# A four-layer graph network on one core: how the Mamba scan gets its B and C rows and its carried state

## The chip, the cores and the metric

The kernel runs on one core of a Trainium2 chip. The metric is the time of one launch in device microseconds; the time before is 3810.78 us, the median of 3 runs (3806.26 to 3815.26). The core's engines run side by side, each through its own queue of instructions in order: TensorE (PE, with its weight loads shown as PEld), VectorE (DVE), ScalarE (ACT), GpSimd (POOL) and SyncE (SP), whose queue issues the DMAs. Semaphores tie the queues together: an instruction waits at the head of its queue until what it needs is there, and all behind it waits with it.

## The reference, cut to what matters

`x` is 3327 x 256, `adj` a sparse 3327 x 3327 matrix of weights. Four layers follow one another, the first three each as `x = layernorm(x + layer(x, adj))`. Layer 0 averages over neighbours and multiplies by W; layer 2 is graph attention; layer 3 makes two passes of diffusion and of attention cut to the top 90%. The change lies in layer 1 and at the seam to layer 2:

```python
h = relu(adj @ x @ gcn_w + gcn_b);  h = layernorm(h) * ln_g + ln_b
xz = h @ w_in;  xc, z = xz[:, :512], xz[:, 512:]
u = silu(causal_conv4(xc) + conv_b)
dbc = u @ w_xp                                   # 16 + 16 + 16 columns
dt = softplus(dbc[:, :16] @ w_dt + b_dt);  B = dbc[:, 16:32];  C = dbc[:, 32:]
dA = exp(dt[:, :, None] * -exp(A_log));  dBu = dt[:, :, None] * B[:, None, :] * u[:, :, None]
# along the 3327 rows:  hst = dA[t] * hst + dBu[t];  ys[t] = hst @ C[t]
y = (ys + u * D_skip) * silu(z);  return y @ w_out
```

The state has 512 channels times 16 states. For each state separately the recurrence is a linear scan along the rows, and `ys` is the sum over the 16 states of `h * C`.

## The kernel before, in words

The 3327 rows are padded to 26 row tiles of 128. Layer 1 has two streams that one program order weaves together.

**The convolution stream** (`convolve`, L254) makes `h` for one row tile after another: 26 matmuls of a 128x128 piece of the transposed adjacency (`at`, loaded nine pieces at a time through two buffers, L263) against all of x, then gcn_w, relu, and three small closures: `measure` (statistics on DVE, then power and nb on POOL, L249, L250, L292), `norm` (ACT, L295) and `turn` (PE transposes, ACT into `hT`, L306). It is a generator. Each `pump` runs one step of it, about nine matmuls, and a step also pops one waiting closure of the tile before.

**The scan** works on channels in the partitions and rows along the free axis, in eight chunks of 128, 256, 384 and five times 512 columns. `head(c)` (L359) makes u, the three-part copy of B and C, dt and du = dt * u for a chunk; it is a generator too and is drawn from during states 3 to 14 of the chunk before. Then, for each of 16 states:

- `decay` (L453): four ACT exponentials (L460) write dA for the four groups of 128 channels, in two buffers; POOL copies the carried state into column 0 of `db` (L458).
- `feed` (L463): one DVE multiplication db = du * B, 128x2048.
- `scan` (L468): one DVE scan over the four groups at once, each led by a column with dA = 0 and db = the carried state, so that it restarts there; POOL copies the last columns to `carry` (L476).
- the multiplication h * C on DVE (L549), with C in PSUM, and four PE matmuls by the identity (L557) that add the product to `ys` in PSUM.

The order on DVE is scan(s), feed(s+1), multiply(s). B and C lie in `dbc` with the state in the partition, while DVE needs them copied to all 128 partitions. The kernel does this on PE: B and C are split into three bf16 parts whose sum is the fp32 value (`parts`, L389, L393, L398, L407), and a matmul with a 0/1 selector `three` (L445 for B, two states ahead; L484 for C) adds the parts and spreads them. B goes by ACT from PSUM to SBUF (`row`, L448); C is read in PSUM. The row matmul, the projections (L355), the dt matmuls (L402), the transposes and the residual all share one PSUM pool of two buffers, `ps`.

After a chunk, `gate` (L491) multiplies `ys` by silu(z), and `back` (L493) multiplies by w_out, adds the residual X0 (L504) and normalizes the chunk's row tiles (POOL L249, L250, L509, L510; ACT L514). `values` (L335) then makes, per row tile, what layer 2 needs: the projection and `F`, the attention columns `col` (L347). For the last chunk all of `back` runs, then the remaining `values`.

Layer 2 (L675 to L757) takes `col`, makes exponentials (`q`, `eps`, `r`), and for each row tile loads two halves of `at` (L724), makes weights on DVE (L726, L729) and multiplies on PE (L732). A runtime branch stands ahead of it. Layer 3 follows; its pass 1 takes diffusion matmuls with `at` (L811, L813) and scores from q and k (L797).

Instructions are put into the engines' queues by a scheduler in program order with readiness, except where `keep_in_program_order` or `high_priority` stands; it also moves loads ahead where their buffers are free.

Of the kernel before, what the change touches and what calls it, by code (L numbers as in the profile page):

```python
# [18 lines left out]
P = 128  # L19
# [24 lines left out]
def gnn_kernel(ctx: ExitStack, tc: tile.TileContext, n: int, a: dict, out: bass.AP):  # L44
# [109 lines left out]
    with tc.tile_pool(name="l1b", bufs=1) as wpool, tc.tile_pool(name="l1at", bufs=2) as l1at:  # L154
# [33 lines left out]
        with tc.tile_pool(name="l1aw", bufs=1) as cwork, tc.tile_pool(name="l1c", bufs=2) as ch, \  # L188
                tc.tile_pool(name="l1t", bufs=3) as tmp, tc.tile_pool(name="l1s", bufs=2) as work, \
                tc.tile_pool(name="l1y", bufs=1, space=PSUM) as ypsum, \  # L190
                tc.tile_pool(name="l1p", bufs=2, space=PSUM) as psum, \
# [5 lines left out]
            w_dt = wpool.tile([6 * DS + DTR, DI], F32, name="w_dt")  # L197
            gb, one = w_dt[0:1, :D], w_dt[0:1, D:D + P]
# [19 lines left out]
            BC = 2 * DS  # L218
            w_sp = wpool.tile([P, NG, 3 * BC + DTR], F32, name="w_sp")
            nc.sync.dma_start(w_dt[3 * BC:, :], a["w_dt"])  # L220
            three = wpool.tile([3 * BC, BC], BF16, name="three")
            for k in range(3):
                nc.sync.dma_start(w_sp[:, :, k * BC:(k + 1) * BC], a["w_xp"][:, :, DTR:])
                nc.vector.tensor_copy(three[k * BC:(k + 1) * BC, :], ident[k * BC:(k + 1) * BC, k * BC:(k + 1) * BC])
            nc.sync.dma_start(w_sp[:, :, 3 * BC:], a["w_xp"][:, :, :DTR])

# [18 lines left out]
            hTs, us, szs, splits = {}, {}, {}, {}  # L245
# [6 lines left out]
            def convolve():  # L252
# [3 lines left out]
                for it in range(nt):  # L256
# [14 lines left out]
                    if rest:  # L271
                        rest.pop(0)()
                        full += 1
                    yield full
# [33 lines left out]
                    rest = [measure, norm, turn]  # L308
# [50 lines left out]
            def head(c):  # L359
# [3 lines left out]


# [20 lines left out]
                for g in range(NG):  # L385
                    nc.tensor.matmul(ps[:3 * BC + DTR, :w], w_sp[:, g, :], u[:, g, :],
                                     start=(g == 0), stop=(g == NG - 1))
                parts = splits[c] = ch.tile([3 * BC, WC], BF16, name="parts")[:, :w]
                nc.scalar.copy(parts, ps[:3 * BC, :w])  # L389
                left = scratch()[:3 * BC + DTR, 0, :w]  # L390
                nc.scalar.copy(left, ps[:3 * BC + DTR, :w])
                yield None
                nc.vector.tensor_sub(left[:3 * BC], left[:3 * BC], parts)  # L393
# [3 lines left out]
                for k in (1, 2):  # L397
                    nc.scalar.copy(parts[k * BC:(k + 1) * BC], left[k * BC:(k + 1) * BC])  # L398
                v, e = (scratch()[:, :, :w] for _ in range(2))
                for g in range(NG):  # L400
                    ps = psum.tile([P, WC], F32, name="ps")
# [174 lines left out]
            for _ in back(nch - 1):  # L576
                pass
# [785 lines left out]
```

## Time and profile before

| what | us |
|---|---|
| median of 3 runs | 3810.78 |
| profiled execution | 3813.28 |
| its span | 3811.5 |
| layer 1's scan: first scan starts | 406.5 |
| scans of chunks 1 to 7 start | 489.6, 603.0, 753.1, 934.5, 1116.5, 1298.7, 1473.1 |
| last multiplication by C ends | 1616.4 |
| first matmul of layer 2 | 1657.4 |
| first matmul of layer 3, pass 1 | 1994.5 |
| pass 2 | 2835.7 to the end |

The profile's lines of the timeline give start, duration, engine, source line, operation, output and inputs with their shapes, and in brackets how long the engine stood idle before and what released it. The table of stages gives the busy time of each engine in a stretch of the span, then the granted clock of TensorE, the busy share of the DMA engines and GB/s. The list of waits gives, for an engine and a line, who released it, total us, times and the longest one.

### The profile page before, as it was taken

Reading aid. Unit: us, or ns where it says so; the run is one execution under the profiler, and the core shown is the slowest. Engines: PE = TensorE matmul, PEld = TensorE weight load, DVE = VectorE, ACT = ScalarE, POOL = GpSimd, SP = SyncE. Lnnn points to the kernel's source line nnn. Section 1 sums busy time; section 2 is a strip of 40 time slices with the busy share of each in tenths; the row PEclk is TensorE's granted clock in tenths of the full one; section 3 lists DMA queues with packets and bytes.
Section 4 is the critical chain, followed back from the end, with each engine's and each line's share of the span. In section 5 each row is a group of like instructions: output and inputs, shape, how many; then the busy total and the mean of one; then the engine's idle time right before and its main releaser. Section 6 shows DMA issues by size and latency. Waiting matters only on the chain. (4 is left out here: it accounts for less than half of the span.)

```text
span 3811.5 us, 42006 instructions
## 1 busy us (share of the span) xinstructions
PE 3482.6 (91%) x15079; PEld 2570.3 (67%) x15079; DVE 2626.2 (69%) x5640; ACT 1739.7 (46%) x2612; POOL 497.9 (13%) x760
## 2 busy tenths in 40 slices
PE   8999999888989778689999999999999899999995
PEld 7888876554545334368877777777777676666764
DVE  1111588898989899957755444444442999999996
ACT  0000655554545465311113333333335878877773
POOL 0000122222212222111110000000000111111111
PEclk9999999998989888889999999999999999999997
DMA  7442221110111000034422221122112222222210
GB/s 230 144 136 96 78 64 50 43 42 31 42 36 43 12 0 0 0 133 141 149 90 74 63 60 52 55 63 60 53 55 61 64 65 61 63 63 61 63 51 7
DMA packets 115508, 252.99 MB, mean 66 GB/s; under 512 B 16450, under 2 KB 57410, under 8 KB 115154
## 3 DMA queue, kind: packets, MB, share of 16 engines
q1 hardware_dynamic: 115282, 250.14, 21.5%
q8 instruction: 122, 2.00, 0.2%
q14 instruction: 104, 0.85, 0.1%
HBM read 239.86 MB, written 10.22 MB: 66 GB/s over the span
## 5 line engine op out<-in xcount | busy, mean ns | idle before, releaser
L473 DVE TENSOR_TENSOR_SCAN h<-dA,db 128x2052 f32<-128x2052 f32 (+3 forms) x128 | 463.8, 3624 | 6.0 <-PE y L557 3.5
L460 ACT ACTIVATE dA<-dt,A_log 128x512 f32<-128x512 f32 (+3 forms) x512 | 296.3, 635 | 331.6 <-DVE h L473 277.8
L557 PE MATMUL y<-h,ident 128*128 128x512 f32 (+3 forms) x1024 | 436.9, 564 | 3.2 <-DVE h L549 3.2
L557 PEld LDWEIGHTS y<-h,ident 128*128 128x128 f32 x1024 | 200.7, 208 | 251.3 <-issue 225.6
L846 PE MATMUL acc<-G,wt 128*128 128x256 f32 x1352 | 345.7, 397 | 11.7 <-ACT wt L782 11.2
L846 PE MATMUL acc<-X,wt 128*128 128x256 f32 x1352 | 343.6, 391 | 8.3 <-ACT wt L844 8.0
L813 PE MATMUL acc<-F,at 128*128 128x256 f32 x1352 | 339.3, 380 | 1.7 <-ACT q L604 0.6
L846 PEld LDWEIGHTS acc<-G,wt 128*128 128x128 f32 x1352 | 247.2, 193 | 112.3 <-ACT wt L782 46.2
L116 PE MATMUL acc<-xa,at 128*128 128x257 f32 x1352 | 309.9, 383 | 5.8 <-DMA at<-in_adjT 5.7
L813 PE MATMUL acc<-X,at 128*128 128x256 f32 x1352 | 309.5, 382 | 3.0 <-issue 2.8
L846 PEld LDWEIGHTS acc<-X,wt 128*128 128x128 f32 x1352 | 242.5, 189 | 103.2 <-issue 41.3
L732 PE MATMUL acc<-F,at 128*128 128x257 f32 x1352 | 307.3, 384 | 4.9 <-DVE at L729 4.9
L264 PE MATMUL cb<-F,at 128*128 128x256 f32 x1352 | 309.6, 381 | 1.6 <-ACT hn L283 1.6
L466 DVE TENSOR_TENSOR db<-du,row 128x2048 f32<-128x2048 f32 (+3 forms) x128 | 240.0, 1878 | 84.3 <-ACT row L448 84.1
L858 DVE MAX8 cand<-e 128x8 f32<-128x128 f32 x676 | 142.1, 278 | 226.2 <-ACT e L799 214.6
L264 PEld LDWEIGHTS cb<-F,at 128*128 128x128 f32 x1352 | 256.5, 191 | 58.6 <-issue 17.6
L116 PEld LDWEIGHTS acc<-xa,at 128*128 128x128 f32 x1352 | 256.5, 191 | 43.3 <-issue 6.2
L732 PEld LDWEIGHTS acc<-F,at 128*128 128x128 f32 x1352 | 255.9, 192 | 41.6 <-issue 5.2
L813 PEld LDWEIGHTS acc<-X,at 128*128 128x128 f32 x1352 | 253.7, 191 | 43.2 <-issue 10.2
L813 PEld LDWEIGHTS acc<-F,at 128*128 128x128 f32 x1352 | 243.2, 190 | 39.2 <-issue 7.8
L549 DVE TENSOR_TENSOR h<-h,C 128x2048 f32<-128x2048 f32 (+3 forms) x128 | 240.8, 1881 | 38.2 <-PE C L484 25.2
L797 PE MATMUL sc<-kT,q 64*128 64x416 f32 x832 | 201.5, 561 | 37.7 <-ACT e L782 34.3
(308 smaller groups left out, 5320.0 us busy)
## 6 DMA issues: line engine op xcount, KB each, us to landing
at<-in_adjT SPq DMA_DIRECT2D x102, 832.0 KB, 4.5
at<-in_adjT SPq DMA_DIRECT2D x260, 320.0 KB, 3.0
at<-in_adjT SPq DMA_DIRECT2D x52, 576.0 KB, 3.7
at<-in_adjT SPq DMA_DIRECT2D x26, 512.0 KB, 3.6
xt<-in_xT SPq DMA_DIRECT2D x26, 128.0 KB, 4.1
qd<-q SPq DMA_DIRECT2D x104, 32.0 KB, 1.9
q<-qd SPq DMA_DIRECT2D x52, 64.0 KB, 1.9
at<-in_adjT SPq DMA_DIRECT2D x52, 64.0 KB, 1.8
```

The costliest lines, as they stand in the source:

```text
L116: nc.tensor.matmul(acc, at[:, j, :], rhs[:, j0 + j, :], start=(j0 + j == 0), stop=(j0 + j == nt - 1))
L264: nc.tensor.matmul(acc, at[:, j % JC, :], X0[:, j, :], start=(j == 0), stop=(j == nt - 1))
L460: nc.scalar.activation(dA[:, g, 1:], dt[:, g, :], AF.Exp, scale=A[:, g, s:s + 1])
L466: nc.vector.tensor_mul(by_group(dbs[s % 2], w)[:, :, 1:], du, B.to_broadcast([P, NG, w]))
L473: nc.vector.tensor_tensor_scan(h[:, :m], dAs[s % 2][:, :m], dbs[s % 2][:, :m], initial=0.0, op0=ALU.mult, op1=ALU.add)
L549: nc.vector.tensor_mul(h, h, C.to_broadcast([P, NG, w]))
L557: nc.tensor.matmul(ys[g][:, :w], ident, h[:, g, :], start=False, stop=(s == DS - 1))
L732: nc.tensor.matmul(acc, at[:, j, :], F[:, j0 + j, :], start=(j0 + j == 0), stop=(j0 + j == nt - 1))
L797: nc.tensor.matmul(pl[:, h, :w], q[k, :], kT[p][k, c0:c0 + w], start=True, stop=True)
L813: nc.tensor.matmul(acc, at[:, j, :], rhs[:, j0 + j, :], start=(j0 + j == 0), stop=(j0 + j == nt - 1))
L846: nc.tensor.matmul(acc, wt[:, j, :], rhs[:, j0 + j, :], start=(j0 + j == 0), stop=(j0 + j == nt - 1))
L858: nc.vector.max(cand[:, s * 8:(s + 1) * 8], z[:, s * SEG:(s + 1) * SEG])
```

## The change

1. **Rows.** `dbc` is copied once from PSUM to SBUF (`left`), and B and C are written to a DRAM tile. For each state one DMA fetches the state's B row and C row to all partitions, into one of three buffers (`lines`), issued two states ahead. The three-part split, the selector matmuls, the copy by ACT and the PSUM bank of C go; the shared PSUM pool has three buffers.
2. **Carried state.** `du` has one more column in front of each group, into which ACT copies the carried state; column 0 of the B row is 1, so that the feed writes it to `db`. ACT copies the last columns out. The scan works in place in `db`, which has three buffers.
3. **Weights of dt** stand four times at partitions 0, 32, 64, 96, and the dt matmuls go in pairs with high priority.
4. **Convolved tiles.** An empty closure is put in ahead of `norm`, and a fourth closure is popped per tile, behind the yield that follows the copy of `acc` (L270); norm comes one step later than before, and turn too.
5. **Last chunk.** Residual, statistics, power and normalization go by row tile, and `values` of the tiles before stand between.
6. **Layer 2.** The `at` pieces of row tile 0 have tiles of their own and are loaded ahead of the preparation; the pool has four buffers in place of five.

Cut to its core:

```diff
                 tc.tile_pool(name="l1y", bufs=1, space=PSUM) as ypsum, \
-                tc.tile_pool(name="l1p", bufs=2, space=PSUM) as psum, \
+                tc.tile_pool(name="l1p", bufs=3, space=PSUM) as psum, \
+                tc.tile_pool(name="l1d", bufs=1, space=DRAM) as l1d, \
                 tc.tile_pool(name="l1q", bufs=1, space=PSUM) as cpsum:
...
             nc.vector.memset(last, 0.0)
-            BC = 2 * DS
-            w_sp = wpool.tile([P, NG, 3 * BC + DTR], F32, name="w_sp")
-            nc.sync.dma_start(w_dt[3 * BC:, :], a["w_dt"])
-            three = wpool.tile([3 * BC, BC], BF16, name="three")
-            for k in range(3):
-                nc.sync.dma_start(w_sp[:, :, k * BC:(k + 1) * BC], a["w_xp"][:, :, DTR:])
-                nc.vector.tensor_copy(three[k * BC:(k + 1) * BC, :], ident[k * BC:(k + 1) * BC, k * BC:(k + 1) * BC])
-            nc.sync.dma_start(w_sp[:, :, 3 * BC:], a["w_xp"][:, :, :DTR])
+            w_sp = wpool.tile([P, NG, 32 * (NG - 1) + DTR], F32, name="w_sp")
+            nc.vector.memset(w_sp, 0.0)
+            for g in range(NG):
+                nc.sync.dma_start(w_dt[32 * g:32 * g + DTR, :P], a["w_dt"][:, g * P:(g + 1) * P])
+                nc.sync.dma_start(w_sp[:, :, 32 * g:32 * g + DTR], a["w_xp"][:, :, :DTR])
+            for k in range(2):
+                nc.sync.dma_start(w_sp[:, :, 32 * k + DTR:32 * k + DTR + DS],
+                                  a["w_xp"][:, :, DTR + k * DS:DTR + (k + 1) * DS])
...
                         rest.pop(0)()
+                    yield full
+                    if rest:
+                        rest.pop(0)()
                         full += 1
-                    yield full
                     for k in range(2):
...
                                                  scale=g1[:, k:k + 1], bias=b1[:, k:k + 1])
-                    rest = [measure, norm, turn]
+                    rest = [measure, lambda: None, norm, turn]
                     while it == 0 and rest:
...
                 for g in range(NG):
-                    nc.tensor.matmul(ps[:3 * BC + DTR, :w], w_sp[:, g, :], u[:, g, :],
+                    nc.tensor.matmul(ps[:w_sp.shape[2], :w], w_sp[:, g, :], u[:, g, :],
                                      start=(g == 0), stop=(g == NG - 1))
-                parts = splits[c] = ch.tile([3 * BC, WC], BF16, name="parts")[:, :w]
-                nc.scalar.copy(parts, ps[:3 * BC, :w])
-                left = scratch()[:3 * BC + DTR, 0, :w]
-                nc.scalar.copy(left, ps[:3 * BC + DTR, :w])
+                left = scratch()[:w_sp.shape[2], 0, :w]
+                nc.scalar.copy(left, ps[:w_sp.shape[2], :w])
+                bc = rows_of[c] = l1d.tile([2, DS, w], F32, name=f"bc{c}")
+                for k in range(2):
+                    nc.sync.dma_start(bc[k], left[32 * k + DTR:32 * k + DTR + DS])
                 yield None
-                nc.vector.tensor_sub(left[:3 * BC], left[:3 * BC], parts)
-                yield None
-                for k in (1, 2):
-                    nc.scalar.copy(parts[k * BC:(k + 1) * BC], left[k * BC:(k + 1) * BC])
                 v, e = (scratch()[:, :, :w] for _ in range(2))
-                for g in range(NG):
-                    ps = psum.tile([P, WC], F32, name="ps")
-                    nc.tensor.matmul(ps[:, :w], w_dt[3 * BC:, g * P:(g + 1) * P], left[3 * BC:],
-                                     start=True, stop=True)
-                    nc.scalar.activation(v[:, g, :], ps[:, :w], AF.Identity, bias=b_dt[:, g:g + 1])
-                    nc.scalar.activation(e[:, g, :], ps[:, :w], AF.Abs, bias=b_dt[:, g:g + 1])
-                yield None
-                nc.vector.tensor_sub(parts[2 * BC:], left[2 * BC:3 * BC], parts[2 * BC:])
+                for g0 in range(0, NG, 2):
+                    pair = [psum.tile([P, WC], F32, name="ps") for _ in range(2)]
+                    with tc.high_priority():
+                        for g, ps in enumerate(pair, g0):
+                            k = slice(32 * g, 32 * g + DTR)
+                            nc.tensor.matmul(ps[:, :w], w_dt[k, :P], left[k], start=True, stop=True)
+                    for g, ps in enumerate(pair, g0):
+                        nc.scalar.activation(v[:, g, :], ps[:, :w], AF.Identity, bias=b_dt[:, g:g + 1])
+                        nc.scalar.activation(e[:, g, :], ps[:, :w], AF.Abs, bias=b_dt[:, g:g + 1])
+                    yield None
                 nc.scalar.activation(e, e, AF.Exp, scale=-1.0)
...
                 nc.vector.scalar_tensor_tensor(dt, v, 0.0, e1, op0=ALU.max, op1=ALU.add)
-                du = ch.tile([P, NG, WC], F32, name="du", bufs=1)[:, :, :w]
-                nc.vector.tensor_mul(du, dt, u)
+                du = by_group(ch.tile([P, NG * (1 + WC)], F32, name="du", bufs=1), w)
+                nc.vector.tensor_mul(du[:, :, 1:], dt, u)
                 for g in range(NG):
...
                 nc.scalar.copy(szs[c][:, g, :], project(c, NG + g, w))
-            dAs, dbs = ([cwork.tile([P, NG * (1 + WC)], F32, name=f"{x}{i}") for i in range(2)] for x in ("dA", "db"))
+            dAs, dbs = ([cwork.tile([P, NG * (1 + WC)], F32, name=f"{x}{i}") for i in range(m)]
+                        for x, m in (("dA", 2), ("db", 3)))
             def by_group(t, w):
                 return t[:, :NG * (1 + w)].rearrange("p (g w) -> p g w", g=NG)
+            lines = [cwork.tile([P, 2, 1 + WC], F32, name=f"row{i}") for i in range(3)]
+            for r in lines:
+                nc.vector.memset(r[:, 0, 0:1], 1.0)
             def row(c, s):
-                parts = splits[c]
-                w = parts.shape[1]
-                pb = psum.tile([P, WC], F32, name="ps")[:, :w]
-                with tc.high_priority():
-                    nc.tensor.matmul(pb, three[:, s:s + 1].to_broadcast([3 * BC, P]), parts, start=True, stop=True)
-                B = work.tile([P, 1, WC], F32, name="row", bufs=2)[:, :, :w]
-                with tc.high_priority():
-                    nc.scalar.copy(B[:, 0, :], pb)
-                return B
+                w = us[c].shape[2]
+                r = lines[(c * DS + s) % 3][:, :, :1 + w]
+                nc.sync.dma_start(r[:, :, 1:], rows_of[c][None, :, s, :].to_broadcast([P, 2, w]))
+                return r
             def decay(x, s):
...
                 w = dt.shape[2]
-                dA, db = (by_group(x[s % 2], w) for x in (dAs, dbs))
+                dA = by_group(dAs[s % 2], w)
                 if s < 2 and (c == 0 or w != ends[c - 1] - starts[c - 1]):
                     nc.gpsimd.memset(dA[:, :, 0:1], 0.0)
-                nc.gpsimd.tensor_copy(db[:, :, 0], carry[:, s, :])
                 for g in range(NG):
                     nc.scalar.activation(dA[:, g, 1:], dt[:, g, :], AF.Exp, scale=A[:, g, s:s + 1])
+                nc.scalar.copy(du[:, :, 0], carry[:, s, :])
             def feed(x, s, B):
                 du = x[2]
-                w = du.shape[2]
-                nc.vector.tensor_mul(by_group(dbs[s % 2], w)[:, :, 1:], du, B.to_broadcast([P, NG, w]))
+                w = du.shape[2] - 1
+                tc.keep_in_program_order(nc.vector.tensor_mul(
+                    by_group(dbs[(x[0] * DS + s) % 3], w), du, B[:, 0:1, :].to_broadcast([P, NG, 1 + w])))
             def scan(x, s):
-                w = x[2].shape[2]
-                h = work.tile([P, NG * (1 + WC)], F32, name="h")
+                w = x[1].shape[2]
+                h = dbs[(x[0] * DS + s) % 3]
                 m = NG * (1 + w)
-                nc.vector.tensor_tensor_scan(h[:, :m], dAs[s % 2][:, :m], dbs[s % 2][:, :m],
+                nc.vector.tensor_tensor_scan(h[:, :m], dAs[s % 2][:, :m], h[:, :m],
                                              initial=0.0, op0=ALU.mult, op1=ALU.add)
                 h = by_group(h, w)
-                nc.gpsimd.tensor_copy(carry[:, s, :], h[:, :, w])
+                nc.scalar.copy(carry[:, s, :], h[:, :, w])
                 return h[:, :, 1:]
-            def reader(x, s):
-                parts = splits[x[0]]
-                w = parts.shape[1]
-                C = cpsum.tile([P, 1, WC], F32, name="C")[:, :, :w]
-                nc.tensor.matmul(C[:, 0, :], three[:, DS + s:DS + s + 1].to_broadcast([3 * BC, P]), parts,
-                                 start=True, stop=True)
-                return C
             def gate(c, ys):
...
                     nc.vector.tensor_mul(sz[:, g, :], ys[g][:, :sz.shape[2]], sz[:, g, :])
+            def residual(c, i):
+                it = starts[c] // P + i
+                po = psum.tile([P, WC], F32, name="ps")[:, :D]
+                for g in range(NG):
+                    nc.tensor.matmul(po, szs[c][:, g, i * P:(i + 1) * P], w_out[:, g, :],
+                                     start=(g == 0), stop=(g == NG - 1))
+                nc.vector.tensor_add(X[:, it, :], X0[:, it, :], po)
             def back(c):
-                sz = szs[c]
-                m = sz.shape[2] // P
+                m = szs[c].shape[2] // P
                 mv = small.tile([P, WC // P, 2], F32, name="mvc")
                 for i in range(m):
...
+                    residual(c, i)
+                    stats(mv[:, i, :], X[:, starts[c] // P + i, :])
                 rs = small.tile([P, WC // P], F32, name="rsc")
...
             decay(x, 0)
-            feed(x, 0, rows.pop(0))
-            C = reader(x, 0)
+            feed(x, 0, rows[0])
             ys = ahead = None
...
                     if nxt:
-                        feed(*nxt, rows.pop(0))
-                    nc.vector.tensor_mul(h, h, C.to_broadcast([P, NG, w]))
-                    if nxt:
-                        C = reader(*nxt)
+                        feed(*nxt, rows[1])
+                    nc.vector.tensor_mul(h, h, rows.pop(0)[:, 1:2, 1:].to_broadcast([P, NG, w]))
                     if s == 0:
...
             gate(nch - 1, ys)
-            for _ in back(nch - 1):
-                pass
+            for i in range(us[nch - 1].shape[2] // P):
+                it = starts[nch - 1] // P + i
+                residual(nch - 1, i)
+                mv = small.tile([P, 2], F32, name="mv")
+                stats(mv, X[:, it, :])
+                rs, nb = (small.tile([P, 1], F32, name=x) for x in ("rs", "nb"))
+                power(rs, mv[:, 1:2])
+                nc.gpsimd.tensor_scalar(nb, mv[:, 0:1], rs, -1.0, op0=ALU.mult, op1=ALU.mult)
+                nc.scalar.activation(X[:, it, :], X[:, it, :], AF.Identity, scale=rs, bias=nb)
+                while valued < ready:
+                    values()
+                ready = it + 1
             while valued < nt:
...
             fit = cpool.tile([1, 1], I32, name="fit")
+            ats = [cpool.tile([P, min(JH, nt - j0), P], F32, name=f"at{j0}") for j0 in range(0, nt, JH)]
+            for k, at in enumerate(ats):
+                nc.sync.dma_start(at, a["adjT"][0][:, k * JH:k * JH + at.shape[1], :])
             with tc.tile_pool(name="l2a", bufs=1) as wpool, \
...
                 with tc.tile_pool(name="l2", bufs=1) as pool, tc.tile_pool(name="l2w", bufs=2) as work, \
-                        tc.tile_pool(name="l2at", bufs=5) as atp, \
+                        tc.tile_pool(name="l2at", bufs=4) as atp, \
                         tc.tile_pool(name="l2p", bufs=3, space=PSUM) as psum:
...
                             m = min(JH, nt - j0)
-                            at = atp.tile([P, JH, P], F32, name="at")
-                            nc.sync.dma_start(at[:, :m, :], a["adjT"][it][:, j0:j0 + m, :])
+                            if it:
+                                at = atp.tile([P, JH, P], F32, name="at")
+                                nc.sync.dma_start(at[:, :m, :], a["adjT"][it][:, j0:j0 + m, :])
+                            else:
+                                at = ats[j0 // JH]
                             w = work.tile([P, JH, P], F32, name="w", bufs=1)
```

## The prediction, made before the changed kernel was run

> **What bounds the kernel now.** I read the table of stages first (busy time of each engine between the scan starts of the eight chunks), because the diff touches layer 1's scan and the two seams behind it. The whole span is no guide: PE is busy for 91% of it, but not here. Chunk 4 and the last chunk:
>
> ```profile
> 934.50:1116.50 182.00, 159.56 (x494) 90.49 (x494) 165.86 (x92) 92.94 (x148) 43.35 (x50) 0.93 0.13 38
> ...
> 1473.10:1616.40 143.30, 106.94 (x261) 51.19 (x259) 141.25 (x63) 60.57 (x118) 29.84 (x34) 0.88 0.00 0
> ```
>
> The columns are length, then PE, weight load, DVE, ACT, POOL. In chunk 4 DVE has the most work (165.86 of 182.00) and stands idle for 16.1 us; in the last chunk it is idle for 2. Over all eight (406.5 to 1616.4) the idle times are 29.8, 24.1, 18.9, 16.3, 16.1, 16.3, 10.4 and 2.1: 134 us. What ends them is in DVE's waits over that stretch:
>
> ```profile
> DVE db L466 <- ACT row L448: 84.1, 22, 12.9
> DVE h L549 <- PE C L484: 25.2, 10, 6.9
> DVE h L549 <- POOL carry L476: 9.2, 21, 1.6
> DVE h L473 <- PE y L557: 3.5, 4, 2.4
> ```
>
> The numbers are total us, times, longest. The first three, 118.5 us, wait for just what the change replaces. DVE's timeline shows the longest one, in chunk 4:
>
> ```profile
> 1062.05 2.29 DVE L549 TENSOR_TENSOR h<-h,C 128x2048 f32<-128x2048 f32 x1 [0.35 <-POOL carry L476]
> 1077.25 4.58 DVE L466 TENSOR_TENSOR db<-du,row 128x2048 f32<-128x2048 f32 x2 [12.92 <-ACT row L448]
> 1081.75 4.43 DVE L473 TENSOR_TENSOR_SCAN h<-dA,db 128x2052 f32<-128x2052 f32 x1
> ```
>
> The feed stood for 12.92 us. PE had only two shared PSUM buffers: ACT was at L404/L405 and waited for the dt matmuls L402, and the row's matmul got its buffer at 1075.96. Such a stall comes once per 512-column chunk with a head behind it. Undisturbed, the loop is DVE's alone, as in the last chunk:
>
> ```profile
> 1576.02 4.43 DVE L473 TENSOR_TENSOR_SCAN h<-dA,db 128x2052 f32<-128x2052 f32 x1
> 1580.36 2.27 DVE L466 TENSOR_TENSOR db<-du,row 128x2048 f32<-128x2048 f32 x1
> 1582.71 2.29 DVE L549 TENSOR_TENSOR h<-h,C 128x2048 f32<-128x2048 f32 x1
> 1584.91 4.43 DVE L473 TENSOR_TENSOR_SCAN h<-dA,db 128x2052 f32<-128x2052 f32 x1
> ```
>
> 8.90 us from scan to scan, and the change keeps those three instructions.
>
> **Rows by DMA.** Removed from PE: 16 row and 16 C matmuls per chunk, 437 + 411 ns at 512 columns (13.6 us; 11.4, 9.7 and 7.2 in chunks 2, 1, 0). From ACT: 16 row copies of 0.58 and three casts (.564 + 2 x .615), 11.1 us. From DVE: two subtractions, 1.36. Put in: per chunk two small writes to DRAM, and per state one broadcast read of 2 rows to 128 partitions, 512 KB in packets of 2 KB. No row of before shows this transfer. From below: 256 packets on 16 engines at the 88 ns that 2 KB packets took are 1.4 us; from above, the loads of 512 KB landed after 3.6 us, 832 KB after 4.5, a broadcast of 128 KB after 4.4 to 5.1. I take 4. It is issued two states ahead, when mult(s-1) frees its buffer: up to feed(s+2) there lie scan, feed, mult, scan, 4.35 + 2.34 + 2.20 + 4.35 = 13.2 us (a quarter of it at 128 columns, by the sizes, where PE is the bound). So it hides, with 9 us over. DMA engines were .10 to .13 busy here; 54.5 MB are added. On SP's queue the rows stand among convolve's `at` loads; By SP's waits it stood there 439 us for a free buffer, 32.6 at the longest, and a row issued behind such a wait is late. That stays as a range end.
>
> By this the 84.1 and the 25.2 us go. What is late next is ACT.
>
> **Carry on ACT.** Removed: POOL's copies. Added to ACT: two copies 128x4 per state; nearest row is ACT's copy 128x2, 161 ns, so 0.16 to 0.2, 6.4 us per chunk. ACT gains more than it gives: 92.9 - 11.1 + 6.4 = 88 of some 168 us. What counts is order. mult(s) now waits for ACT's copy of scan(s)'s last column, feed(s+1) for the copy into du. Behind the scan lies the feed, so the carry copy has 2.27 us before mult stands; the du copy follows the four exps (2.6 us) that start when scan(s-1) ends, and has 8.9. Between two carry copies in the new ACT order lie 3.0 to 8.9 us of work, 10.8 in one state of a chunk and 12 at a chunk change that lasts 14. Against 8.9 + 2.27 that fits unless ACT itself waits. Bounds: zero, and from above ACT's waits for PE and POOL in this stretch, of which the largest is
>
> ```profile
> ACT hn L295 <- POOL nb L292: 46.1, 11, 6.1
> ```
>
> (with `t`, `sz`, `hn` L283, `X`, `col` and `m` 146 us). The change puts a step between measure and norm, 8.9 us against the longest 6.1, so the 46 should go; the rest are short (2 to 5 us) and begin inside the slack. I take 4 us of idle time per 512-column chunk, about the 0.4 us of "POOL carry" now at a few states.
>
> POOL's rs took 222 ns at the median and 4.9 us at the longest, longer than a scan. The Trainium skill ("SBUF — State Buffer", "Who interferes with whom") says that a DVE instruction with two SBUF inputs contends with a GpSimd instruction that reads SBUF. The multiply is the one instruction of the three whose second input lies in PSUM, and the change moves it to SBUF. By the rule three POOL operations of a tile could each be held for a scan (estimate 13 us), still inside the two steps now left to them; were they not, 25 tiles by one multiply each would be 57 us. My sum goes by the first.
>
> **Turn one step later.** 108 steps in place of 107; one more is forced in chunk 0, where PE is the bound: +3.6 us (a nine-tile group of 381 ns). Elsewhere the step lies beside DVE.
>
> **dt matmuls in pairs, three PSUM buffers, w_sp and w_dt copied four times**: the same matmuls, 112 columns as before, six more small loads under layer 0. Nothing; the third buffer takes the place of C.
>
> **Sum for layer 1.** A chunk cannot be shorter than its busier engine:
> - chunk 0: PE 79.7 - 7.2 + 3.6 = 76; now 83.1; with the present gap of 3.4, 79: -4
> - chunk 1: PE 104.6 - 9.7 = 95, DVE 88; now 113.4; both near, so 100: -13
> - chunk 2: PE 139.9 - 11.4 = 128.5, DVE 130; now 150.1; two engines level; of the present gap to PE, 10.3, I keep 8: 138: -12
> - chunks 3 to 5: DVE 164.5, PE 143 to 149; now 181.9; 164.5 + 4 = 168.5: -40 together
> - chunk 6: DVE 162.6 + 4; now 174.4: -8
> - chunk 7: 0; head of chunk 0 before its first scan: -1 (casts and row copies at 128 columns)
>
> That makes -78 (-111 if DVE and PE never waited).
>
> **Into layer 2.** After the last multiply (1616.37) came gate, residual and statistics of four tiles, one normalization, then values, 2.98 us per tile (1632.6 to 1646). By tile, values of one tile lie beside the residual of the next: PE's 17.6 us of work from 1622.3 end at about 1641, -5. The first `at` then landed late:
>
> ```profile
> 1655.36 1.89 DVE L729 SCALAR_TENSOR_TENSOR at<-at,w 128x1664 f32<-128x1664 f32 x1 [3.96 <-DMA at<-in_adjT]
> ```
>
> It is now issued at values' end, not behind it: that wait goes, -4. Four `at` buffers for five: PE is 320 of 337 us busy there, nothing.
>
> **Into layer 3.** The new tiles take the room in which U2, ln3 and the first three `at` loads of layer 3 were fetched early (`at` at 1622); now they are issued behind layer 2, among the q loads, and pass 1 is PE's (832.5 of 841.2). PE had 5.65 us of diffusion matmuls to do before q came: +5 (0 to 8).
>
> Total: -78 - 9 + 5 = -82. The profiled execution took 3813.3 (span 3811.5): 3731. The median of the runs, 3810.78, lies 2.5 lower, so I say 3730.
>
> **Rivals.**
> 1. PE or the step order takes half (0.25). Chunks 1 to 5 lose only half of their 65 us, since PE stood at 143 to 149 of 168 with its own y matmuls bound to mult, and rows behind `at` waits: 3763. For it: PE waits 44 us on DVE for C now, and its clock is .93. Against: those waits vanish with C.
> 2. Nothing waits at all (0.12): the floors, -111 - 9 + 5: 3698. Against: levels in chunks 1 and 2.
> 3. Slower (0.08): ACT's carry copy late at mult. Place: mult(s), slack 2.27. Price: all of the 146 us of ACT's waits land on DVE: 3730 + 146 = 3876. It decides from 82 us on, 0.73 us in each of 112 states. Against: 88 us of ACT work in 168.
> 4. No change (0.05): the same lateness at half price, 73 us: 3803; or row transfers that land 14 us after issue rather than 4, each further us costing 104.
>
> My forecast has 0.50 (3710 to 3750). The range takes in rivals 1 and 2 to their near parts: 3695 to 3780. A difference of 0.2% (7.6 us) is about what a measurement of this kernel can tell from none: faster 0.87, same 0.05, slower 0.08.
>
> **What would show it.** Right: no wait on row L448 or C in DVE's list; chunks 3 to 5 at 166 to 172; feed ended by no DMA; last multiply at about 1538, layer 2's first matmul 32 us behind it. Wrong: DVE waiting for ACT `carry` or `du` by more than 10 us per chunk, or for a row's DMA; PE over 95% in chunks 3 to 5; POOL nb holding ACT; layer 3 entering with a DMA wait over 8 us.

## The result and the profile after

The changed kernel takes 3747.81 us (median of 4 runs, 3747.03 to 3750.36), the kernel before 3808.52 in the same sitting (4 runs). The ratio is 0.984, with a 95% interval of 0.9823 to 0.9857. The prediction was 3730, with a range of 3695 to 3780: the sign and the range hold, the named waits went, and the gain is 61 us where 81 was forecast. The profiled execution shows where (spans 3811.5 and 3748.6; each stage from its first to the next one's first instruction; 1616.4, which the table of before calls the end of the last multiplication by C, is its start):

| stage | before | after | change | forecast |
|---|---|---|---|---|
| layer 0, to its last tile's degree | 360.3 | 354.2 | -6.1 | 0 |
| from there to the first scan | 46.2 | 40.6 | -5.6 | -1 |
| chunks 0, 1, 2 | 83.1, 113.4, 150.1 | 82.4, 110.3, 141.2 | -0.7, -3.1, -8.9 | -4, -13, -12 |
| chunks 3, 4, 5 | 181.4, 182.0, 182.3 | 175.5, 174.6, 174.6 | -21.0 | -40 |
| chunk 6; chunk 7 to the start of its last multiply | 174.3; 143.3 | 166.6; 145.0 | -7.7; +1.7 | -8; 0 |
| start of the last multiply to layer 2's first matmul | 41.0 | 31.8 | -9.2 | -9 |
| layer 2 | 325.2 | 321.4 | -3.8 | 0 |
| layer 2's last matmul to the end | 1828.9 | 1830.4 | +1.5 | +5 |

The eight chunks gave 39.7 us and not 77; layer 0 and the head before the first scan gave 11.7 and not 1. Layer 2 differs by more than 3.8 us between runs with the same layer 2 (318 to 331), so that row says nothing. In the chunks DVE was busy for 1075.8 us before and 1067.8 after, and idle for 134.1 and 102.4: most of the gain is idle time, but far less of it than the 109 us of waits that went.

DVE's list of waits over layer 1's scan (380 to 1570, so with some of the head ahead of it) answers to the one of before:

```profile
DVE db L470 <- PE y L553: 34.5, 15, 6.0
DVE db L547 <- ACT carry L481: 26.7, 40, 3.3
DVE u L379 <- ACT u L374: 16.6, 12, 2.0
DVE db L470 <- ACT du L464: 9.9, 7, 3.4
...
DVE db L470 <- DMA row<-bc: 1.2, 1, 1.2
```

The waits for the row's copy (84.1) and for C (25.2) are gone, as forecast, and rows by DMA cost one wait of 1.2 us. In their place stand others: for PE's y, for ACT's carry copy, for ACT's first convolution tap u. The table of stages, chunk 4 and the last chunk (cut 1.6 us short of the last multiply):

```profile
904.20:1078.80 174.60, 150.03 (x465) 88.43 (x464) 164.73 (x89) 86.69 (x161) 25.68 (x18) 0.92 0.32 88
...
1420.00:1563.40 143.40, 100.88 (x228) 48.57 (x228) 139.05 (x62) 56.70 (x134) 7.69 (x4) 0.85 0.19 48
```

DVE is busy for 164.73 us of chunk 4, as the sum had it (164.5), and idle for 9.9; the sum had 4. The longest single wait in chunk 4 is worth following, since one cause runs through four engines. DVE, ACT and POOL, in three timelines:

```profile
939.51 2.27 DVE L470 TENSOR_TENSOR db<-du,row 128x2052 f32<-128x2052 f32 x1
945.04 2.29 DVE L547 TENSOR_TENSOR db<-db,row 128x2048 f32<-128x2048 f32 x1 [3.26 <-ACT carry L481]
```
```profile
943.34 1.58 ACT L513 ACTIVATE X<-X,nbc,rsc 128x256 f32<-128x256 f32 x3 [10.46 <-POOL nbc L509]
944.83 0.18 ACT L481 COPY carry<-db 128x4 f32<-128x4 f32 x1
```
```profile
935.36 4.27 POOL L251 TENSOR_SCALAR rsc<-mvc 128x4 f32<-128x4 f32 x1 [25.30 <-DVE mvc L85]
939.71 2.97 POOL L252 TENSOR_TENSOR rsc<-rsc,mhalf 128x4 f32<-128x4 f32 x1
```

The multiply L547 waits for the carry copy; the carry copy stands on ACT behind three normalizations X of the chunk before (one per row tile, with a scale rsc and a bias nbc that POOL makes from the statistics mvc); these wait for POOL's nbc; and POOL's first operation on that chain takes 4.27 us, from just after the scan starts (935.20, on DVE's timeline) to its end (939.60). The same operation took 1.9 us at the median before and 4.3 after. Before, in 5 of 7 chunks, it began with the feed, which is half as long as a scan, and the carry copy was POOL's and not behind X on ACT:

```profile
960.68 2.25 DVE L466 TENSOR_TENSOR db<-du,row 128x2048 f32<-128x2048 f32 x1
```
```profile
960.84 2.19 POOL L249 TENSOR_SCALAR rsc<-mvc 128x4 f32<-128x4 f32 x1 [0.37 <-DVE mvc L85]
```

After, it began with the scan in 6 of 7. ACT's waits for nbc over the whole scan, before and after:

```profile
ACT X L514 <- POOL nbc L510: 13.5, 6, 4.1
```
```profile
ACT X L513 <- POOL nbc L509: 52.3, 6, 10.5
```

### The profile page after: what moved, and what is told of

It is laid out like the page before. It is cut to its first block, busy times and chain, and to the rows that moved or that the text cites. A ratio compares the mean times of both kernels' runs of the same rounds, so it can differ in the third digit from the quotient of the medians.

```text
span 3748.6 us, 41470 instructions
## 1 busy us (share of the span) xinstructions
PE 3410.7 (91%) x14823; PEld 2539.4 (68%) x14823; DVE 2616.3 (70%) x5625; ACT 1700.0 (45%) x2716; POOL 403.7 (11%) x512
## 5 line engine op out<-in xcount | busy, mean ns | idle before, releaser
L553 PE MATMUL y<-db,ident 128*128 128x512 f32 (+3 forms) x1024 | 439.2, 572 | 63.1 <-DVE db L547 63.1
L478 DVE TENSOR_TENSOR_SCAN db<-dA,db 128x2052 f32<-128x2052 f32 (+3 forms) x128 | 463.7, 3623 | 0.9
L553 PEld LDWEIGHTS y<-db,ident 128*128 128x128 f32 x1024 | 199.2, 209 | 255.4 <-issue 157.1
L470 DVE TENSOR_TENSOR db<-du,row 128x2052 f32<-128x2052 f32 (+3 forms) x128 | 241.0, 1883 | 46.7 <-PE y L553 34.5
L547 DVE TENSOR_TENSOR db<-db,row 128x2048 f32<-128x2048 f32 (+3 forms) x128 | 241.2, 1885 | 26.7 <-ACT carry L481 26.7
```

The lines of the kernel that those rows point to most:

```text
L470: tc.keep_in_program_order(nc.vector.tensor_mul(by_group(dbs[(x[0] * DS + s) % 3], w), du, B[:, 0:1, :].to_broadcast([P, NG, 1 + w])))
L478: nc.vector.tensor_tensor_scan(h[:, :m], dAs[s % 2][:, :m], h[:, :m], initial=0.0, op0=ALU.mult, op1=ALU.add)
L547: nc.vector.tensor_mul(h, h, rows.pop(0)[:, 1:2, 1:].to_broadcast([P, NG, w]))
L553: nc.tensor.matmul(ys[g][:, :w], ident, h[:, g, :], start=False, stop=(s == DS - 1))
```

## The experiments

Each run is compared with the kernel before on the same chip; the changed kernel's own ratio is 0.984. Its 3747.81 us come from another sitting than the runs, but each of their three sittings has a run within 2.2 us of it (3749.94, 3748.39 and 3749.89 in runs 1, 8 and 9), so the times may be compared too. Stage lengths are read from each run's one trace, as in the table. In traces that share the changed kernel's scan (runs 1, 8, 9, 11) all chunks together take 1166.9 to 1170.6 us (1170.2 in the table) and chunk 3 alone 172.6 to 175.2: differences of that size show nothing.

**1. A finished chunk's normalization, drawn a state later**

```diff
-                    if s in (0, 4) and c:
+                    if s in (0, 5) and c:
```

> The changed kernel with one edit: a finished chunk's normalization is drawn at state 5 and not at state 4. Theory (engine order): in each chunk ACT stands at the first normalization X for POOL's nbc, whose rsc is held while DVE scans; the carry copy behind it on ACT is late and the multiply waits 3.3 us (1.4 to 1.9 in the small chunks). A state later POOL is done: that wait goes, 15 to 20 us less than the changed kernel, about 3730. Rival (PE and the order of the convolution steps set the length of a chunk): the 3.3 us come back as another wait; within 4 us of 3748.

Measured: 3749.94, ratio 0.9849 (0.9833 to 0.9866). DVE's wait for the carry is 26.6 us in 40 pieces, as in the changed kernel, and the order on DVE and POOL did not change at all. On ACT three of the four X still stood ahead of state 3's carry copy: only the first of them is pinned in program order, and the scheduler moves the other three forward. So this run does not speak on the theory; run 5 does.

**2. The carry copied out by POOL**

```diff
-                nc.scalar.copy(carry[:, s, :], h[:, :, w])
+                nc.gpsimd.tensor_copy(carry[:, s, :], h[:, :, w])
```

> The changed kernel with the carry copied out of the scan by POOL, as before; the copy into du stays on ACT. Theory (POOL is held by DVE instructions that read two SBUF operands, now all three of a state): the copy starts with the feed and is often held until the feed ends, and POOL's power operations ahead of it are held by scans; the multiply waits at many states, 10 to 40 us more than 3748. Rival (POOL's copy fits into the 2.27 us of the feed as before, where its wait was 9 us in all): 3740 to 3750.

Measured: 3767.08, ratio 0.9893 (0.9877 to 0.991), 19 us above the changed kernel; the chunks hold 14.6 of it. The theory's sign and size hold; the rival's 3740 to 3750 does not. The multiply's waits:

```profile
DVE db L547 <- POOL carry L481: 32.0, 58, 1.7
```

That is 58 of them, against ACT's 40 with 26.7 us. Chunks 0 to 2 grew by 3.9, 2.7 and 2.4 and chunks 4 and 5 by 3.5 and 2.2.

**3. Two buffers in the shared PSUM pool**

```diff
-                tc.tile_pool(name="l1p", bufs=3, space=PSUM) as psum, \
+                tc.tile_pool(name="l1p", bufs=2, space=PSUM) as psum, \
```

> The changed kernel with two buffers in the shared PSUM pool, as before. Theory (the row's matmul and copy left that pool, and with them DVE's dependence on it): 0 to 6 us more than 3748, and no DVE wait over 4 us in chunks 3 to 5. Rival (two buffers were the cause of the 12.9 us stalls): 30 to 60 us more, the stalls coming back behind other work of ACT or PE.

Measured: 3753.46, ratio 0.9853 (0.9837 to 0.987); the chunks are 2.2 us longer in all, and no DVE wait in chunks 3 to 5 is over 3.3. So without the row's passage through that pool two buffers do not bring the 12.9 us stalls back, and the third is worth little. Whether a third buffer would have cured them with the row still in the pool, no run shows.

**4. The convolution's closures as before**

```diff
                     if rest:
                         rest.pop(0)()
+                        full += 1
                     yield full
-                    if rest:
-                        rest.pop(0)()
-                        full += 1
...
-                    rest = [measure, lambda: None, norm, turn]
+                    rest = [measure, norm, turn]
```

> The changed kernel with the convolution's closures as before: measure, norm, turn without the empty one, and without the pop behind the yield. Theory (ACT's norm waits for POOL, which is now held longer, and the carry copy stands behind it): ACT waits for nb 40 to 80 us and 15 to 40 of it reach DVE: 3763 to 3790. Rival (the carry copy has 2.27 us of room and ACT's waits for nb begin inside it; one PE step less in chunk 0): 3742 to 3752.

Measured: 3755.76, ratio 0.9864 (0.9847 to 0.988). ACT does wait:

```profile
ACT hn L297 <- POOL nb L294: 67.2, 14, 10.8
```

But the chunks are only 8.6 us longer in all: 12 more in chunks 1 and 2 (116.1 and 147.4), and nothing clear in the others. The theory was right on the wait and put what gets through too high: 15 us at the least, 8 measured.

**5. All four normalizations pinned behind state 4's carry copy**

```diff
-                    if i == 0:
-                        tc.keep_in_program_order(x)
+                    tc.keep_in_program_order(x)
```

> The changed kernel with all four normalizations X of a finished chunk pinned behind state 4's carry copy in ACT's order (before, only the first was pinned, and up to three were queued ahead of state 3's carry copy; drawing them a state later did not move them). Theory (engine order): the multiply no longer waits for ACT's carry copy behind POOL's nbc: 3.3 us less in each of chunks 4 to 6, 1 to 2 in chunks 2 and 3, 10 to 15 us less in all, about 3736. Rival (the length of a chunk is set elsewhere): the time comes back as waits for PE's y or ACT's u; within 4 us of 3748.

Measured: 3738.81, ratio 0.9814 (0.9788 to 0.9839): 9 us less than the changed kernel's 3747.81. DVE's wait for the carry falls from 26.7 to 10.2 us. Chunks 4 and 6 are 171.0 and 162.0 long, where the changed kernel has 174.6 and 166.6; chunk 5 is 177.1: there ACT still stood 8.9 us for nbc, now at state 5, and run 6 takes that away.

**6. The same, drawn a state later** (edits 1 and 5 together)

> The changed kernel with the four normalizations pinned in ACT's order, as in the run that pinned them at state 4, and drawn at state 5. Theory (one chunk of that run still had ACT standing 8.9 us for POOL's nbc, and its fifth state was late by 5): that wait goes as well, 3 to 6 us less than with the pin at state 4, 3732 to 3736. Rival (what is left is PE's y and ACT's u): 3738.

Measured: 3732.6 (3725.89 to 3739.13), ratio 0.98 (0.9783 to 0.9817). Chunks 4, 5 and 6 are 171.0, 171.1 and 163.2. This is faster than both kernels, by 15 us against the changed one; its 6 us against run 5 lie within the spread of the two runs' times (3730.58 to 3739.3 there) and are seen in chunk 5. DVE is idle for 84.6 us in the chunks where the changed kernel has 102.4. On ACT the carry copy now goes first:

```profile
952.34 0.20 ACT L481 COPY carry<-db 128x4 f32<-128x4 f32 x1 [2.74 <-DVE db L478]
952.44 2.07 ACT L513 ACTIVATE X<-X,nbc,rsc 128x256 f32<-128x256 f32 x4
```

What is left on DVE:

```profile
DVE db L470 <- PE y L552: 36.8, 18, 6.0
DVE u L379 <- ACT u L374: 16.3, 12, 2.0
DVE db L546 <- ACT carry L481: 10.0, 34, 1.4
```

The rival's waits, PE's y and ACT's u, are there unchanged: they are real, but they are not where the 3.3 us had come from or went.

**7. Each row fetched twice**

```diff
-                nc.sync.dma_start(r[:, :, 1:], rows_of[c][None, :, s, :].to_broadcast([P, 2, w]))
+                for _ in range(2):
+                    nc.sync.dma_start(r[:, :, 1:], rows_of[c][None, :, s, :].to_broadcast([P, 2, w]))
```

> The changed kernel with the row transfer of every state issued twice, the second over the first. Theory (a row lands 4.9 us after issue and has 13 us): two land in some 8 us; nothing in chunks 3 to 7, up to 3 us each in the chunks of 128 and 256 columns: 3748 to 3756. Rival (rows are near their limit by SP's queue or DMA traffic): DVE's feed waits for rows in most states, 3780 or more.

Measured: 3781.95, ratio 0.9936 (0.9913 to 0.9959), 34 us more, the rival's number. But not the rival's place: chunks 0 and 1 grew by 21.0 and 11.7 us, chunk 2 by 0.6, and chunks 3 to 7 not at all (170.8, 174.5, 174.2, 166.6, 145.0). In the stretch 397 to 500.4, chunk 0 of this run, DVE waited

```profile
DVE db L471 <- DMA row<-bc: 24.5, 8, 5.1
DVE db L471 <- PE y L554: 19.9, 5, 8.3
```

and from 622.4 to 1450.3 no wait for a row is on its list. The DMA list of the changed kernel's page says why the small chunks pay:

```profile
row<-bc SPq DMA_DIRECT2D x80, 512.0 KB, 4.9
...
row<-bc SPq DMA_DIRECT2D x16, 384.0 KB, 4.8
row<-bc SPq DMA_DIRECT2D x16, 256.0 KB, 5.0
```

The landing time does not fall with the size; 16 rows of 128 KB took 5.0 us too. The two transfers went one behind the other: SP's queue waited for a landed row before it went on, 59.5 us in 15 waits in chunk 0 (397 to 500). A state of chunk 0 lasts 82.4 / 16 = 5.2 us, one of chunk 4 10.9. Two landings in a row, some 10 us, fit into the lead of the large chunks and not into that of the small ones; the rows by themselves had room.

**8. Layer 2 without the early at**

```diff
-            ats = [...]
...
-                        tc.tile_pool(name="l2at", bufs=4) as atp, \
+                        tc.tile_pool(name="l2at", bufs=5) as atp, \
-                            if it:
...
+                            at = atp.tile([P, JH, P], F32, name="at")
+                            nc.sync.dma_start(at[:, :m, :], a["adjT"][it][:, j0:j0 + m, :])
```

> The changed kernel with layer 2 as before: five at buffers, nothing loaded ahead. Theory (a trade): the entry to layer 2 loses the 4 us of the late first at, and some 4 us inside layer 2; layer 3 has its first loads early again and wins 5 to 6 at its entry; 3746 to 3754. Rival (the late at was hidden anyway and only the loss in layer 3 is real): 3742.

Measured: 3748.39, ratio 0.9849 (0.9825 to 0.9872). The trade is even: the entry to layer 2 takes 36.5 us instead of 31.8, the rest behind layer 2's last matmul is 3.4 us shorter. The changed kernel's PE at layer 3's entry:

```profile
1926.20 1.22 PE L607 MATMUL ps<-xt,wkq 128*128 128x128 f32 x4 [0.52 <-ACT xt L103]
1935.94 1.76 PE L811 MATMUL sc<-kT,q 64*128 64x416 f32 x4 [8.51 <-DMA at<-in_adjT]
```

Before, 14 diffusion matmuls of 5.65 us stood in that gap, with `at` there early.

**9. The last chunk finished as before**

```diff
-            for i in range(us[nch - 1].shape[2] // P):
-                it = starts[nch - 1] // P + i
-                residual(nch - 1, i)
...
-                ready = it + 1
+            for _ in back(nch - 1):
+                pass
```

> The changed kernel with the last chunk finished as before: residual and statistics of all four tiles, one normalization, then values. Theory: from the last multiply to the first matmul of layer 2 some 37 us instead of 31.8, 5 us more than 3748. Rival (the early at alone made the 9 us): 32, the same time.

Measured: 3749.89, ratio 0.984 (0.9824 to 0.9857). In the trace the entry to layer 2 takes 35.0 us, 3.2 more; in the run's time that does not show. With run 8's 4.7 this makes 7.9 of the 9.2 us, by the traces.

**10. Rows by DMA with the rest undone** (edits 2, 3, 4, 8 and 9 together; the scan in place, the carry copied into du by ACT and the paired dt matmuls stay)

> The changed kernel with everything undone but the rows by DMA, the in-place scan and the copy into du: POOL copies the carry out, two PSUM buffers, the old closures, the last chunk by back and then values, layer 2 as before. Theory (the rows are the gain, and what was measured for each other part adds up: 17 + 8 + 4 + 5 for the last chunk + 0): 3775 to 3788, and no DVE wait of 12 us. Rival (the parts hide the same idle time and undoing all costs no more than the dearest): 3765 to 3772. Second rival (rows alone do not pay; the parts need each other): 3795 or more.

Measured: 3785.68, ratio 0.994 (0.9923 to 0.9956): in the theory's window. The surprise is in its parts. The eight chunks take 1201.7 us against 1209.9 before: rows alone win 8 us there, and chunks 4 and 5 (183.3 and 181.4) win nothing. DVE's list:

```profile
DVE db L468 <- PE y L551: 56.8, 15, 10.1
DVE db L545 <- POOL carry L479: 28.5, 53, 1.9
```

And ACT's:

```profile
ACT hn L297 <- POOL nb L294: 84.0, 16, 11.6
ACT du L462 <- DVE db L468: 58.4, 40, 4.6
ACT X L511 <- POOL nbc L507: 52.5, 6, 9.7
```

The 109 us of waits for row and C went, and some 100 us of others came: DVE is idle for 128.5 us in the chunks, against 134.1 before. 28.5 us are POOL's carry; how much of the 56.8 for y stands behind POOL as well, by the multiply ahead of it, was not told apart. The rest of this run's gain lies ahead of the scan (layer 0 6.7, head 4.1) and around layer 2.

**11 and 12. Layer 0's 6 us.** No part of the change is in layer 0. Before, its fourth and fifth tile took 17.5 and 15.7 us, in the changed kernel 13.25 each, as most others in both. DVE's and PE's timelines and the table of stages (clock in the third column from the end) of the kernel before:

```profile
63.95 0.43 DVE L234 SCALAR_TENSOR_TENSOR t<-wg,t 128x256 f32<-128x256 f32 x1 [4.85 <-DMA t<-in_attn_dst]
```
```profile
65.58 0.69 PE L101 MATMUL ps<-ident,m 128*128 128x128 f32 x2 [3.96 <-DVE m L175]
```
```profile
64.70:80.40 15.70, 14.82 (x58) 12.58 (x59) 2.38 (x11) 1.95 (x3) 0.08 (x1) 0.80 0.37 133
80.40:93.60 13.20, 13.20 (x63) 11.51 (x62) 2.40 (x8) 0.67 (x2) 0.00 (x0) 1.00 0.44 141
```

Four setup products of attn_src and attn_dst were put into DVE's queue ahead of the fourth tile's degree; DVE stood for their loads, PE stood 4 us behind DVE, and the next tile ran at a granted clock of 0.80. The changed kernel issues more small loads for w_dt and w_sp ahead of these, and the scheduler put the first pair of products one tile's normalization later. Two runs test it. In the changed kernel, the block was written ahead of the loads of w_sp:

```diff
+            wg = wpool.tile([P, 2, D + 2], F32, name="wg")
+            nc.sync.dma_start(wg[:, :, :D], a["gat_w"])
+            for k, v in enumerate(("attn_src", "attn_dst")):
...
             w_sp = wpool.tile([P, NG, 32 * (NG - 1) + DTR], F32, name="w_sp")
...
-            wg = wpool.tile([P, 2, D + 2], F32, name="wg")
...
```

> The changed kernel with the four setup products of attn_src and attn_dst written ahead of the loads of w_sp; the order of PE, ACT and POOL is the same, on DVE the four products stand ahead of the fourth tile's degree again, as before. Theory (that order made layer 0 6 us longer before, since DVE stood for two loads, PE stood 4 us behind it and ran at a clock of .80 after): 3 to 6 us more than 3748. Rival (layer 0's 6 us had another cause): within 2 us of 3748.

Measured: 3748.65, ratio 0.9844 (0.9821 to 0.9867), layer 0 ends at 353.4. The 3 to 6 us of the theory did not come: the products did stand ahead of the degree, but their loads were issued earlier too and landed at 59.5 and not 63.95, just before the tile's sums (60.3). Order alone is not the cause. In the kernel before, the same block was written ahead of the loads of w_dt and w_sp. The order on PE, ACT and POOL is the same, on DVE too but for one small operation on A_log:

```diff
+            wg = wpool.tile([P, 2, D + 2], F32, name="wg")
...
             BC = 2 * DS
             w_sp = wpool.tile([P, NG, 3 * BC + DTR], F32, name="w_sp")
...
-            wg = wpool.tile([P, 2, D + 2], F32, name="wg")
...
```

> The kernel before with the block that loads attn_src and attn_dst and makes the four products written ahead of the loads of w_dt and w_sp; PE, ACT and POOL have the same order. Theory (layer 0 was 6.05 us longer before because the late loads of this block held DVE, DVE held PE for 4.0 us and the clock after it was .80): the loads land some 4 us earlier, the fourth and fifth tile take 13.25 us instead of 17.5 and 15.7, layer 0 ends near 354: 6 us less than before. Rival (other cause): layer 0 ends at 360.

Measured: 3800.89, ratio 0.9984 (0.9975 to 0.9994); layer 0 ends at 354.5, the fourth and fifth tile take 14.5 and 13.1. The loads landed at 60.76 and not 63.95. That is the theory's number: 5.8 us of layer 0 were a load that came late to a queue in which the next tile stood behind it. So some 6 of the change's 61 us could be had in the kernel before by moving this block.

## Why the prediction was right, and where it was off

- **The waits for row and C go: right.** 84.1 and 25.2 us before, none after. Rows hide behind the scan as worked out: 4.9 us to landing where 4 was taken, one wait of 1.2 us.
- **"I take 4 us of idle time per 512-column chunk": the term that was mis-sized.** Measured: 10 to 11 us in chunks 3 to 5. It was sized by the POOL waits of before, the wrong row: what counted was what stood right behind the big waits. Of the difference the carry copy behind X and POOL is some 3.3 us per chunk: runs 5 and 6 took it away (chunks of 171), and 6.4 us are left in chunks 4 and 5 of run 6. These are mainly waits for u (2.3 us in chunk 4 of the changed kernel) and for y (2.4), which the sum left out. Before, they hardly show (0.2 us for u and 3.5 for y in all chunks); that DVE came late to them because it stood for row and C is an argument, not shown.
- **The named ACT wait was the wrong one.** The prediction saw that ACT could hold the carry copy and bounded it by 146 us, but it followed `hn` on nb, which the added step does cover (no `nb` on ACT's list after), and called `X` on nbc short, 2 to 5 us. X became the largest of ACT's waits for POOL and PE, 52.3 us in 6 pieces, up to 10.5.
- **The rule on POOL holds, and was worked out for one chain of two.** The prediction named the Trainium skill ("SBUF — State Buffer", "Who interferes with whom") and took its rule as covered by two steps. In the trace of before, the 38 carry copies that began during a feed (both inputs in SBUF) took 1.9 us on average, the 34 that began with DVE idle 0.19. The first operation of the chain (rs of a tile, rsc of a chunk) took 0.22 to 0.24 us in all 15 cases in which it began during the multiply, with C in PSUM; after, with C in SBUF, the two that began there took 2.18 and 2.19. For nb it was seven of 0.27 us before and four of 1.4 to 4.4 after. So the multiply was POOL's free window, and the change closed it. The bound the prediction gave holds for nb; it was not worked out for rsc and nbc, which had no such cover. The longest wait itself does not need the closed window: there POOL was held by a scan and then a feed, which had both inputs in SBUF before as well; new are the place where the chain began and the carry copy behind X.
- **Chunks 0 to 2: -29 forecast, -12.7 measured.** In chunk 1 PE was busy for 102.1 us and not the 95 of the sum, though row and C matmuls were gone; its waits for ACT's hn (6.5 us) and DVE's for PE's y (5.8) are new. That PE's busy time fell by 2.4 us where 9.7 were taken out stays unexplained. By lines, with overlaps counted twice, the matmuls' durations fell by 7.7 us (118.4 to 110.7), and some of y's records are missing in the trace of before (122 of 128), so the two sums cannot be compared to the microsecond.
- **Ahead of the scan: -1 forecast, -11.7 measured.** 6.1 are layer 0's late load, which the prediction did not look at: it counted the added loads at nothing. The other 5.6 lie in the head of the first chunk; run 10 keeps 4.1 of them, so they come with what that run keeps: no casts and row matmuls ahead of the first feed, and the dt matmuls in pairs. These were not told apart.
- **The seams: right in sum.** Into layer 2 -5 and -4 were forecast, -9.2 measured; by runs 9 and 8 the parts are 3.2 and 4.7. Into layer 3 +5 was forecast; the two traces of the table give +1.5. Over all traces the stretch behind layer 2's last matmul takes 1830.4 to 1832.7 us with the early at (10 traces) and 1824.6 to 1828.9 without (4), 4.5 more on average.
- **The signs it gave.** Met: no wait for row or C, layer 2's first matmul 32 us behind the last multiply. Not met: chunks 3 to 5 at 166 to 172 (174.6 to 175.5), the last multiply at 1538 (1565), and one feed did wait for a row, 1.2 us. One sign of being wrong appeared, a DMA wait over 8 us at layer 3's entry (8.51); another only in kind: POOL held ACT, by nbc and not by nb.
- **Slips in the sum.** Nine times 381 ns are 3.4 us and not 3.6. ACT gives up more than it gains (11.1 against 6.4), which the 88 has right and the sentence wrong. "After the last multiply (1616.37)" is that multiply's start.

The size came near by luck in part: without the 10.7 us ahead of the scan that were not foreseen, the time would have been some 3758, inside the range but outside the 3710 to 3750 that had half the chance.

Of the rivals, "half the gain" (3763) lies about as near to the result as the forecast. Its mechanism does not hold in chunks 3 to 5: PE did not bound them (150 of 174.6 busy), DVE did, with ACT's queue and POOL behind it as the one cause of idle time that a run took away. In chunks 0 to 2 it may: 26.2 of DVE's 34.5 us of waits for PE's y fall there, and PE is busy for 77.5 of 82.4 and 102.1 of 110.3 us in the first two. No run tests this.

## What to carry to other kernels

A wait that ends last can hide the waits behind it: here 109 us of waits went and DVE's idle time fell by 32. After taking one out, price the engine's next ones by the queue that the waiting instruction stands in, not by the waits that show now. Where a copy moves to an in-order engine, list all that the scheduler may put ahead of it there, and pin what waits for a slow producer; pinning alone was worth 9 us here, pinning it one state later 15. The part that the change is named for can be the smaller one: the rows with little else won 8 us in the scan and 21 in all, some 6 of these layer 0's. Undone one by one, the five other parts cost 19, 6, 8, 1 and 2 us (runs 2, 3, 4, 8, 9), 36 together, and undone at once 38: here they add up. What they would gain without the rows, no run shows.

## What was not expected of the hardware

- A broadcast of a row pair from DRAM to 128 partitions landed after 4.8 to 5.0 us at the median (4.4 to 6.8 over all 128) whether it moved 128 or 512 KB.
- In place and with 2052 columns, feed, multiply and scan cost the same as before, but a state in the last chunk is 8.73 us and not 8.90 (scans at 1551.50 and 1560.23): the multiply starts 2.18 us after the feed (1555.85 and 1558.03), where before 2.35 passed (1580.36 and 1582.71). Why is not shown.
- PE standing idle for 4 us was followed by a tile at a granted clock of 0.80 in place of 1.00, 2.5 us more: that stall cost over half as much again as it lasted. In run 12, where PE stood 0.9 us at most there, the same tile ran at 1.00.
